# The projection and the convolution behind it eight slots later in the last unit of an attention

## Chip, cores and metric

The kernel runs on one core of one Trainium2 chip. The metric is the device time of one execution in microseconds (us); the median of three runs is given.

## What is computed

Four layers follow one another on an input of 2 images, 256 channels, 64 x 64 pixels, all in float32.

```python
x = _L0_conv_ref(x, ...)   # group norm, attention of 4 heads over 4096 pixels, projection, + xn
x = _L1_conv_ref(x, ...)   # + position term
x = _L2_conv_ref(x, ...)   # bottleneck: 1x1 conv, deformable 3x3 conv (mask), 1x1 conv, + x
x = _L3_conv_ref(x, ...)   # group norm, deformable 3x3 conv, group norm, deformable 3x3 conv, + x
```

The attention and the deformable convolution are

```python
scores = jnp.einsum('bhci,bhcj->bhij', q, k) * d ** (-0.5)
attn = jax.nn.softmax(scores, axis=-1)
out = jnp.einsum('bhij,bhcj->bhci', attn, v).reshape(B, C, H, W)
proj = jnp.einsum('bchw,oc->bohw', out, w_proj) + b_proj[None, :, None, None]
...
samp = _bilinear(h, y, x)            # 4 corners for each of 9 taps, gathered by computed offsets
out = jnp.einsum('bckhw,ock->bohw', samp, w.reshape(O, C, 9))
```

## The kernel before

**Units, blocks, slots.** The attention (`attention`, line 181) works on four units: image 0 or 1, first or second pair of heads (`units`, line 243). The last unit is image 1, second pair. A unit has 16 blocks of 256 query pixels, a block 16 slots, and a slot is one piece of work for 128 query pixels, one head and 1024 keys. So the last unit has 256 slots. The loop at line 678 takes two slots a turn. In each it sends to PE the scores of two slots ahead (`scores`, L581), the transposes of the exponentials (`turn`, L611) and the product with the values of four slots back (`attend`, L640). DVE takes the maximum (`lowest`, L593), ACT the exponential (L599); both copy the transposed results (`keep`, L628 and L630) out of two pairs of PSUM tiles.

**The order of the work.** The order on PE, ACT, DVE and POOL is that in which the code issues it. Only SP's queue of transfers is ordered by the scheduler, and a transfer may stand there ahead of those issued before it. Each engine works its queue in order: an instruction that waits holds up all behind it.

**Steps with a slot of their own.** `due(at, f)` puts a step into a slot; `small(n)` runs it there, steps of one slot in the order of their entry. For block i of a unit, with `at = 16i`, the class `Block` (line 447) enters: the softmax shares across four key parts (`compare`, `raised`, `weights`, slots 13 to 15); `spread` (16), where PE transposes the shares (L503), DVE copies them, and SP writes them to memory and reads them back as tile `f` spread over the partitions (L507, L511); and `combine` (20), where POOL multiplies the block's outputs `o` with `f` (L520), adds the parts (L521) and writes half of tile `avs` (L526). In the very last block DVE does that.

**The projection and what follows.** Every odd block also has `fetch` (17), a load of `res`; `project(0)` and `project(1)` (27 and 28), where PE multiplies `avs`, which holds two blocks, with the projection weights (L545) and DVE adds the result to `res` (L556), after which SP stores it in `xa` (L558); and, in units of the second pair of heads, `second_layer` (30): the first 1x1 convolution of the bottleneck (`Bottleneck.first`, L939 on PE, four copies `h` on ACT, L956). `make_q` (L279) stands in slot 18 of every 32 and makes the next queries, with copies to tile `qs` by SP (L289).

**Tiles with one buffer.** `f`, `avs`, `res`, `o` and `pos` have one buffer each (`o` holds the outputs of even blocks, `pos` those of odd blocks in the last unit). All steps of `small` and of the background share one PSUM bank, `pm` (`Bank`, line 43): copies out of it by ACT are put off until the next step asks for the bank or the next turn begins.

**Background.** A slot without a step of its own takes a background step, and each turn one or two more (`background`, line 662). In the last unit these are, in order of precedence: `Bottleneck.before` for image 1 (line 964), which waits until a `second_layer` has run, then makes that part of the image (PE transposes L973, SP stores L983) and the offsets of the part before (L1010, L1041 on PE, some twenty small DVE steps in `corners`, line 732); what is left of image 0's bottleneck and the building of its image (`early_image`, line 1217); and `early_samples` (line 1254), which computes offsets for five blocks of the first deformable convolution and queues 180 gathers.

**Early gathers.** At the end of each turn `self.sample()` (lines 727 and 1292) issues up to two pairs on POOL: a store of a finished gather to memory (L1297) and the next gather (L856), 512 KB each; 15 pairs fall between two combines. `combine` stands among them in POOL's queue.

**After the attention.** `deform` (line 1338) runs the bottleneck's deformable convolution of image 1 beside the first layer of the last convolution. Its loads of `xa` (L919) and of the stored samples (L1485) stand in SP's and POOL's queues.

Of the kernel before, what the change touches and what calls it, by code (L numbers as in the profile page):

```python
# [64 lines left out]
class Net:  # L65
# [115 lines left out]
    def attention(self, bott):  # L181
# [5 lines left out]
        with ExitStack() as ctx:  # L187
# [39 lines left out]
            for i in range(NB):  # L227
# [3 lines left out]
                if i == 1:  # L231
                    for j in range(2):
                        at = slice(64 * j, 64 * j + 5)
# [9 lines left out]
            units = [(b, hp) for b in range(B) for hp in range(2)]  # L243
# [154 lines left out]
            def due(at, f):  # L398
                own.setdefault(at, deque()).append(f)
# [47 lines left out]
            class Block:  # L447
# [3 lines left out]
                def __init__(self, u, i):  # L451
                    self.u, self.i = u, i
                    self.low = work.tile([P, 4, 4], F32, name="low")
                    self.sum = work.tile([P, 4, 4], F32, name="sum")
                    at = u * per_unit + 16 * i
                    due(at + 13, self.compare)
                    due(at + 14, self.raised)
                    due(at + 15, self.weights)
                    due(at + 16, self.spread)
                    due(at + 20, self.combine)  # L460
                    if i % 2:
                        due(at + 17, self.fetch)
                        due(at + 27, lambda: self.project(0))
                        due(at + 28, lambda: self.project(1))
                        if units[u][1] == 1:
                            due(at + 30, self.second_layer)
# [211 lines left out]
            while n < last + 4 or back or more or any(own.values()):  # L678
                u, d = divmod(n, per_unit)
# [1098 lines left out]
```

## Time and profile before

| | |
|---|---|
| median of 3 runs | 5222.68 us (5215.43 to 5223.12) |
| profiled execution | 5255.39 us, its span 5253.6 us |
| PE busy | 4874.5 us, 93% of the span |
| DVE, ACT, POOL busy | 76%, 63%, 47% |
| 2600 to 3075 us: PE, POOL busy | 433 us and 261 us of 475 |
| the same: DMA engines | 96% busy, 348 GB/s |
| transposes of the shares (L503) in the last unit | blocks 4, 5, 7, 9, 11, 13, 14, 15 begin at 2578.2, 2622.7, 2715.5, 2808.3, 2913.8, 3012.3, 3060.3, 3101.4 us |
| last projection (L545) | begins at 3110.6 us |

The profile takes one execution, so its times are set against its own 5255.39 us. A line of the waits names who waited, for whom, and how long in total. In a timeline, the bracket at the end of a line is the idle time before the instruction and what ended it. TensorE's clock is given as the share that was granted.

### The profile page before, as it was taken

How to read it: one execution, taken by the hardware profiler on the slowest of the kernel's cores; microseconds unless marked ns; L12 is line 12 of the kernel's file. 1: busy time of each engine (PE TensorE's matmuls, PEld its weight loads, DVE VectorE, ACT ScalarE, POOL GpSimd, SP SyncE). 2: the span in 40 equal slices, each digit the busy share in tenths (PEclk: the TensorE clock that was granted, in tenths of full speed). 3: DMA queues.
4: the chain of work that ended last, by engine and by line, in shares of the span. 5: the costliest groups of instructions: out<-in, count | busy, mean ns of one | idle time of the engine just before them, and what ended most of it. 6: DMA issues, size and time to landing. Idle time of an engine off the chain costs nothing.

```text
span 5253.6 us, 101327 instructions
## 1 busy us (share of the span) xinstructions
PE 4874.5 (93%) x38680; PEld 2736.0 (52%) x38680; DVE 3977.1 (76%) x7081; ACT 3284.2 (63%) x5941; POOL 2446.4 (47%) x2436
## 2 busy tenths in 40 slices
PE   8999999999999999989998877788999999999998
PEld 5555565555555555555555544444444544444444
DVE  6878767787678888665676757777778888888887
ACT  5676656666566666564566645557866766666665
POOL 0111101111018888622455547774766666666665
PEclk9999999999999999999999988889999999999999
DMA  4221111111113333346799988888989999999998
GB/s 167 64 94 56 44 61 44 49 30 46 50 52 104 103 107 111 102 123 210 266 346 356 343 296 276 283 299 308 345 321 322 371 334 336 336 381 345 341 356 304
DMA packets 398997, 1113.50 MB, mean 212 GB/s; under 512 B 65052, under 2 KB 102490, under 8 KB 398510
## 3 DMA queue, kind: packets, MB, share of 16 engines
q0 software_dynamic: 222480, 784.79, 41.4%
q1 hardware_dynamic: 175486, 322.11, 18.9%
q8 instruction: 303, 4.96, 0.4%
q14 instruction: 184, 1.51, 0.1%
q10 hardware_dynamic: 544, 0.13, 0.0%
HBM read 914.48 MB, written 183.97 MB: 209 GB/s over the span
## 4 chain that ended last, share of the span: by engine, by line
PE 28%; DVE 9%; DMA 8%; issue 4%; ACT 3%; another core or an unknown queue 3%; POOL 2%; DVEq 0%; SPq 0%; ACTq 0%; POOLq 0%
PE out L1564 12%; PE pd L813 4%; PE pt L1545 3%; DVE smp L1533 2%; PE av L640 2%; DVE four L1514 2%; PE sc L581 2%; DMA samp_d<-xb 2%; DMA four<-img,didx 2%; DMA xb<-img,bidx 1%; DVE smp L1527 1%; PE pm L813 1%; PE tt L611 1%; DMA samp_d<-bx 1%
## 5 line engine op out<-in xcount | busy, mean ns | idle before, releaser
L599 ACT ACTIVATE e<-sc,low 128x1024 f32<-128x1024 f32 x1024 | 1147.4, 1120 | 746.5 <-DVE low L593 704.9
L593 DVE TENSOR_REDUCE low<-sc 128x1 f32<-128x1024 f32 x1024 | 1205.3, 1218 | 247.5 <-PE sc L581 226.5
L1564 PE MATMUL out<-st,wc 128*128 128x512 f32 x2304 | 1238.7, 620 | 123.8 <-ACT st L1554 61.2
L856 POOL DMA_INDIRECT four<-img,didx x972 | 1034.5, 1064 | 613.8 <-issue 237.1
L581 PE MATMUL sc<-k,qs 64*128 64x512 f32 x2048 | 1007.4, 611 | 0.3 <-DVE k L368 0.3
L640 PE MATMUL av<-et,v 128*64 128x256 f32 x8192 | 996.1, 385 | 0.0
L581 PE MATMUL sc<-k,q 64*128 64x512 f32 x2048 | 984.7, 610 | 0.0
L611 PEld LDWEIGHTS tt<-ident,e 64*128 64x128 f32 x16384 | 655.0, 140 | 560.6 <-issue 280.1
L630 ACT COPY et<-tt 128x512 f32<-128x512 f32 x1152 | 659.5, 585 | 225.2 <-PE tt L611 164.9
L611 PE MATMUL tt<-ident,e 64*128 64x64 f32 x16384 | 733.5, 227 | 70.4 <-ACT et L630 44.5
L628 DVE COPY et<-tt 128x512 f32<-128x512 f32 x896 | 612.9, 684 | 175.4 <-PE tt L611 166.5
L640 PEld LDWEIGHTS av<-et,v 128*64 128x64 f32 x8192 | 553.1, 137 | 303.5 <-issue 50.5
L856 POOL DMA_INDIRECT bfour<-img,bidx x576 | 610.2, 1059 | 214.9 <-issue 111.8
L1545 PEld LDWEIGHTS pt<-ident,smp 128*128 128x128 f32 x2304 | 332.0, 145 | 664.4 <-issue 551.3
L1533 DVE SCALAR_TENSOR_TENSOR smp<-four,dw,smp 128x256 f32<-128x256 f32 x1296 | 626.3, 483 | 58.5 <-issue 14.3
L520 POOL TENSOR_TENSOR o<-o,f 128x1024 f32<-128x1024 f32 x48 | 113.9, 2374 | 1094.4 <-DVE o L472 542.5
L1564 PEld LDWEIGHTS out<-st,wc 128*128 128x128 f32 x2304 | 390.0, 197 | 362.7 <-issue 245.3
L1514 DVE SCALAR_TENSOR_TENSOR four<-four,dwt 128x512 f32<-128x512 f32 x540 | 403.8, 748 | 173.2 <-ACT four L1508 125.1
L1545 PE MATMUL pt<-ident,smp 128*128 128x128 f32 x2304 | 452.4, 279 | 28.2 <-DVE smp L1527 18.4
L1554 ACT COPY st<-pt 128x1024 f32<-128x1024 f32 x288 | 289.4, 1005 | 297.7 <-PE pt L1545 178.6
L581 PEld LDWEIGHTS sc<-k,qs 64*128 64x128 f32 x2048 | 349.2, 190 | 213.9 <-issue 128.3
L1508 ACT ACTIVATE four<-four,dwt 128x512 f32<-128x512 f32 x540 | 388.2, 719 | 111.6 <-DMA four<-img,didx 96.4
(201 smaller groups left out, 5416.9 us busy)
## 6 DMA issues: line engine op xcount, KB each, us to landing
four<-samp_d SPq DMA_DIRECT2D x172, 512.0 KB
samp_d<-xb POOLq DMA_DIRECT2D x116, 512.0 KB
f<-share_d SPq DMA_DIRECT2D x128, 256.0 KB
xb<-xn SPq DMA_DIRECT2D x55, 512.0 KB
img<-imgt SPq DMA_DIRECT2D x96, 256.0 KB
xa<-res SPq DMA_DIRECT2D x32, 512.0 KB
samp_d<-k POOLq DMA_DIRECT2D x32, 512.0 KB
samp_d<-bx POOLq DMA_DIRECT2D x32, 512.0 KB
```

The costliest lines, as they stand in the source:

```text
L581: nc.tensor.matmul(s[:, j, :], lhsT=q[u, i // 2][int(h != j)][halves[j], at : at + P], rhs=k[u][c][halves[j], h, :], start=True, stop=True,)
L593: nc.vector.tensor_reduce(low, s, AX.X, ALU.max, negate=True)
L599: nc.scalar.activation(e.rearrange("p j n -> p (j n)"), s, AF.Exp, bias=blk.low[:, g, c : c + 1], accum_out=blk.sum[:, g, c : c + 1],)
L611: nc.tensor.transpose(pt[:, m, :], e[half, m // 4, m % 4 * P : m % 4 * P + P], self.ident[half, half],)
L628: nc.vector.tensor_copy(dst, pt)
L630: nc.scalar.copy(dst, pt)
L640: nc.tensor.matmul(now["av"][halves[h], :], lhsT=v[u][c][:, m, halves[h]], rhs=ets[j][:, m, h, :], start=(m == 0), stop=(m == 7),)
L856: self.nc.gpsimd.indirect_dma_start(out=dst, out_offset=None, in_=img, in_offset=bass.IndirectOffsetOnAxis(ap=idx, axis=0),)
L1514: nc.vector.scalar_tensor_tensor(uv, four[:, 2 * C :], share(s, 1, 1), uv, ALU.mult, ALU.add)
L1533: nc.vector.scalar_tensor_tensor(smps[s], four[:, c], weight(s, c), smps[s], ALU.mult, ALU.add)
L1545: nc.tensor.transpose(pts[u][:, c, j * P : (j + 1) * P], smp[:, c * P : c * P + P], self.ident,)
L1564: nc.tensor.matmul(outs[ob], lhsT=wc[k][:, c, ob * P : ob * P + P], rhs=sts[u][:, c, :], start=(k == 0 and c == 0), stop=(k == K2 - 1 and ...
```

## The change

In the last unit, for the odd blocks 1 to 13, `project(0)`, `project(1)` and `second_layer` are entered at slots 35, 36 and 38 of the block instead of 27, 28 and 30. `fetch` stays at 17. Block 15 and the other units are not changed.

```diff
                     if i % 2:
                         due(at + 17, self.fetch)
+                        if u + 1 == len(units) and i < 15:
+                            at += 8
                         due(at + 27, lambda: self.project(0))
                         due(at + 28, lambda: self.project(1))
                         if units[u][1] == 1:
                             due(at + 30, self.second_layer)
```

Since slots with a step of their own take no background step there, the background moves too. Counted from the start of the last unit:

| step | slot before | slot after |
|---|---|---|
| first early offsets ready, first gather | 47 | 45 |
| block 3: project, second_layer, image part 1, offsets of part 0 | 75, 76, 78, 81, 81 to 91 | 83, 84, 86, 87, 88 to 101 |
| block 13: project, second_layer, image part 6, offsets of part 5 | 235, 236, 238, 241, 241 to 251 | 243, 244, 246, 247, 248 to 261 |
| last store of an early gather | 241 | 239 |
| block 15: project, second_layer | 267, 268, 270 | the same |

In SP's queue, the store of `xa` and the next load of `res` now follow the queries' copies (`qs`) and stand ahead of the image's four stores; the shares and `f` of the even blocks come before them.

## Prediction

> **What bounds the kernel now.** I read the list of what PE waited for first, cut to the last half of the attention (2000 to 3110 us). Its columns are us in total, times, longest.
>
> ```profile
> PE pm L545 <- POOL avs L526: 23.1, 4, 10.9
> PE tt L611 <- ACT et L630: 21.4, 22, 4.4
> PE tt L611 <- DVE et L628: 9.7, 7, 3.3
> ```
>
> The moved projection (L545) is itself the largest wait: four times PE stands still until POOL has written `avs` in `combine` (L526). The same list for POOL (2300 to 3110 us) shows why POOL is late:
>
> ```profile
> POOL xb L856 <- DMA samp_d<-xb: 81.3, 88, 3.5
> POOL samp_d L1297 <- DMA xb<-img,bidx: 75.2, 62, 3.0
> ```
>
> POOL's queue holds the 180 early gathers and stores, each waiting for a transfer, with `combine` in between. In the table of stretches (us, PE, PEld, DVE, ACT, POOL, PE clock, DMA share, GB/s) the DMA engines are full:
>
> ```profile
> 2650.00:2700.00 50.00, 45.82 (x483) 27.16 (x479) 37.24 (x57) 31.25 (x59) 27.34 (x34) 0.99 0.98 367
> 2800.00:2850.00 50.00, 38.75 (x423) 22.85 (x421) 27.36 (x39) 27.13 (x52) 28.76 (x36) 0.90 0.96 333
> ```
>
> So from about 2600 to 3075 us the DMA engines set POOL's pace, and POOL sets PE's at every projection. POOL's timeline gives odd combines beginning at 2641.9, 2740.5, 2840.8, 2940.4 and 3037.8 us: 99 us for two blocks (32 slots). PE alone is faster: its transposes of the shares (L503) for blocks 7 and 9 begin at 2715.5 and 2808.3, 92.8 us apart, of which 6.4 are waits, leaving 86.3. PE gains 12 to 13 us on POOL in two blocks and gives it back at L545. The last time it does so, in PE's timeline (start, us, work):
>
> ```profile
> 3036.60 1.95 PE L640 MATMUL av<-et,v 128*64 128x256 f32 x16
> 3042.34 1.08 PE L545 MATMUL pm<-avs,wproj 128*64 128x512 f32 x4 [3.79 <-POOL avs L526]
> 3043.35 0.85 PE L611 MATMUL tt<-ident,e 64*128 64x64 f32 x16
> 3043.99 1.17 PE L581 MATMUL sc<-k,q 64*128 64x512 f32 x1
> ...
> 3101.37 0.30 PE L503 MATMUL pm<-ident,share 128*64 128x128 f32 x1 [0.59 <-DVE share L492]
> ```
>
> and POOL's side of it:
>
> ```profile
> 3037.77 2.37 POOL L520 TENSOR_TENSOR pos<-pos,f 128x1024 f32<-128x1024 f32 x1
> 3040.22 1.26 POOL L521 TENSOR_TENSOR pos<-pos 128x512 f32<-128x512 f32 x1
> 3041.56 0.72 POOL L526 TENSOR_TENSOR avs<-pos 128x256 f32<-128x256 f32 x1
> ```
>
> POOL had no gap before this combine (its last gather ends where it begins), so 3042.3 us is set by the DMA chain, whatever PE does.
>
> **The change, step by step.** Slots count from the start of the last unit.
>
> 1. *The seven moved projections* (blocks 1 to 13) add no instruction. Before, PE cannot pass slot 16i+27 until combine(i) is done; now slot 16i+35. At 3042.3 us PE stands at slot 235 before the change; after it, PE may stand at slot 243. The eight slots between hold eight slots of attention: the pair of slots repeats every 4.79 us in PE's timeline (L640 at 3012.48, 3017.27, 3022.06) and 4.85 a little later, so 4 x 4.83 = 19.3 us. From the anchor to the last L503 (slot 256) PE took 3101.4 - 3042.3 = 59.0 us. After the change 19.3 of these are already spent: the last L503 comes at 3082.1, **19.3 us earlier**. It holds if PE can be at slot 243 by 3042.3. From block 5's L503 (slot 96, 2622.7) it is 147 slots, 4.59 x 86.3 = 396, so 3019: 23 us of room. The stalls on `et` in that stretch (4.42, 2.4, 4.19, 3.88 us at 2700, 2797, 2899, 2998) take 14.9 if they all stay, leaving 8. With two blocks at 89.7, as between blocks 9 and 11 less their waits, 15.6 more goes, PE is 7.5 late, and this step gives 12. I take enough room: 19.3.
>
> 2. *What is late next.* POOL falls up to 15 slots behind its place in the program, 7 before. The next things that hold PE for a late combine are `o`/`pos`, rewritten by DVE for block i+2 some 19 slots after combine's place: four slots are left. `avs` in the other direction: combine(i+1) writes it after project(1) of block i, now in combine's own slot, and before it in that slot. Combines 6, 8 and 10 began at 2692, 2792 and 2891 us, when PE by the rate above is past the projection by over 10 us. I cost it at nothing; if that cover went, POOL would wait at most one projection (1.1 us) in seven blocks.
>
> 3. *The one bank `pm`.* The projection now follows make_q (slots 18, 19 of 32) and the image step follows the second layer (22, 23), so each waits for a copy on ACT put in between. Before, the transpose of the shares paid for the h copies: 3.0 us in five waits, 0.3 to 1.0 each; the next row for a q or k copy is 0.7 us (L503 on ACT k L427). The four h copies take 1.97 us together. Bounds per block are -1.0 (the old wait is gone and the new one hidden by the attend matmuls) and +2.7; I take +0.5, the nearest row being the old wait. All but the last of these fall where PE has room, so 0.5 us counts.
>
> 4. *Background work and POOL.* Of 32 slots, 11 and 12 come free for background steps (14 keeps `raised`) and 19 and 22 are taken (20 already holds combine): as many steps, but ahead of the image they wait for. The early samples' first block is ready at slot 45, not 47, and their last store stands at 239, not 241. POOL waits for PE's products at combines 2 and 3 anyway (14.4 and 26.6 us), so the two pairs done earlier fall off the end: two pairs are 2 x (3075 - 3042)/13, some 5 us. The chain of gathers ends near 3070.
>
> 5. *SP's queue.* Between the f loads of block 13 and 14 stand the first two loads of the later convolution (L919), which wait for the last sample stores:
>
> ```profile
> 3019.97 1.17 SPq L511 DMA_DIRECT2D f<-share_d  x2
> 3078.05 0.38 SPq L919 DMA_DIRECT2D bx<-xa  x1
> 3078.54 0.41 SPq L558 DMA_DIRECT2D xa<-res  x1
> ```
>
> In the new order the shares and f of block 14 come straight behind them, ahead of xa, res and the image. With L919 at 3070, shares 3070.5, f issued 3074 and landed by 3079, combine(14) ends at 3083.5. The shares of block 15 leave at 3083 to 3084, f lands by 3090, DVE's combine takes 2.4 us (1.23 + 0.69 + 0.42 in its rows), and the last projection begins at 3092 to 3093 instead of 3110.6: **18 us earlier**. The unmoved last block means the image, offsets and gathers after it keep their order. A stored xa lands up to eight slots later but is loaded only in the later convolution.
>
> 6. *Other traffic.* Eight slots more of PE's loads and stores fall before the anchor: a quarter of some 3 MB for two blocks, 0.75 MB, at 350 GB/s 2 us, from 0 to 2. I take 1.
>
> Sum: 18 - 0.5 - 1 = 16.5, rounded **17 us**. Everything after the attention hangs on that last projection in the chain of waits, so it moves as a whole. The profiled run took 5255.4 us (span 5253.6): 5238 after. The median of the runs shown is 5222.7, 32.7 below it; I take the same 17 off: **5206 us**.
>
> TensorE's clock speaks for a little more. After the wait of 3.8 us the score matmuls take 1.06 us instead of 0.59; eight of them, two at a time, lose 8 x 0.47 / 2, some 2 us, and the granted clock is 0.90 in the stretch of the longest wait. The Trainium skill, "TensorE: Matmul & The Clock Gate", What's actually happening, says that an idle window of about 3.4 us halves the clock and a busy one restores it. By that rule each such wait that goes away is worth about 1.7 us more, an estimate from that page, and the sum would be 17 to 24; the trace agrees in size. I leave the gain out of the sum: by the 23 us of room, waits may stay at blocks 11 and 13, with their slow stretch.
>
> **Rivals.**
>
> *PE becomes the bound (gain 0 to 10).* DVE's 128x72 steps of the offsets take 0.23 us, and long where they meet POOL's combine:
>
> ```profile
> 2691.52 2.92 DVE L764 TENSOR_TENSOR floor<-floor,whole 128x72 f32<-128x72 f32 x1
> ```
>
> The three long `et` waits follow such meetings. The steps now lie six to ten slots later and POOL seven later, so they meet again, and spread over eight slots instead of four they can meet twice. Twice 14.9 us, with 86.3 for two blocks, overdraws the room by 23.5 - 29.8 = -6: gain 11; with 89.7 as well the gain is nil. The Trainium skill, "SBUF — State Buffer", Who interferes with whom, says that a DVE step with two SBUF inputs and a GpSimd step that reads SBUF shut each other out for a whole instruction. The 2.92 us beside POOL's 2.38 agree; by it this rival costs no more than one combine, 4.4 us, a meeting.
>
> *SP's queue turns into the wait (slower).* `f` has one buffer, so f of block i+1 waits on SP for combine(i), asked for at slot 16i+32. PE may now be three slots past that, and the q copies (qs) stand right behind. They are asked for at slot 19 of 32 and needed at 30: 11 slots, 30 us. f landed 5 to 8 us after its issue at blocks 4 and 14. It decides from a landing of 30 us on; four q blocks 7 us late each lose the 17 and 11 more: 5234. Against it: the longest landing SP itself waited for was 8.9 us.
>
> *The gain is not passed on (0).* The later convolution could be held by something that does not move, such as the sample stores. Against it: these end near 3070. It gives 5223.
>
> *More (22 to 28).* PE meets no late combine at all, and the four slow stretches of some 2 us go too: 17 + 8 = 25, so 5198.
>
> **How the numbers follow.** Forecast (gain 11 to 22) 0.60; PE the bound 0.18; not passed on 0.08; SP's queue 0.09; more 0.05. A measurement of this kernel tells a change from none at about 0.2%, 10.4 us. Faster takes the forecast, the last rival and 0.02 of PE the bound: 0.67. Same takes the rest of that and the case of no gain: 0.24. Slower 0.09. The range leaves out SP's queue and the far half of the last rival; its ends are a gain of 27 and one of 1: 5196 to 5222.
>
> **What would show it.** L545 waits for `avs` under 15 us in all, and later than block 9. The last L503 near 3082, the last L545 near 3093, the last sample store near 3070, combines still 99 us apart by two blocks. PE's wait on `et` growing past 25 us would mean the first rival, a wait of L581 on `qs` the second. If combines change pace, the DMA chain was not the bound and the anchor is wrong.

## The result, and the profile after

The median of eight executions of the changed kernel is 5202.0 us (5183.9 to 5209.7), that of the kernel before in the same set 5222.9 us (5214.5 to 5235.6). The ratio is 0.996, interval 0.9948 to 0.9973: 20.9 us less. In a second set the same pair gave 0.9956 (0.9942 to 0.9969), 20.8 us less. The profiled execution took 5197.2 us, its span 5195.3.

The two profiled executions differ by 58 us, almost three times what the medians do. Only part of that is the change: the last projection (L545 before, L547 after, the new code being two lines further down) begins at 3110.6 us before and 3087.8 after, 22.8 us earlier. Behind it the one took 2143.0 us and the other 2107.5, but another profiled execution of the unchanged kernel took 2111.0 there. So the 22.8 us are read below, and the rest is left alone.

PE's waits after the change, 2000 to 3110 us (us in total, times, longest):

```profile
PE tt L613 <- ACT et L632: 14.4, 20, 2.2
PE pm L547 <- POOL avs L528: 10.2, 2, 5.8
PE pm L975 <- ACT h L958: 9.6, 7, 1.7
PE tt L613 <- DVE et L630: 8.3, 8, 1.7
```

The wait of the projection for POOL is down from 23.1 to 10.2 us, in two places instead of four: it is gone at blocks 7 and 9 and left at 11 and 13. The waits for `et` fell (31.1 to 22.7 us in all) instead of growing. A new line is the image step (L975), which waits for the copies `h`.

The same two stretches as in the prediction (us, PE, PEld, DVE, ACT, POOL, PE clock, DMA share, GB/s):

```profile
2650.00:2700.00 50.00, 48.68 (x513) 28.42 (x510) 32.30 (x49) 33.91 (x65) 26.86 (x32) 1.00 1.00 360
2800.00:2850.00 50.00, 50.00 (x557) 29.67 (x555) 38.03 (x57) 35.08 (x66) 27.99 (x35) 1.00 0.97 352
```

PE is full where it was busy 38.75 of 50 us, its granted clock there is 1.00 instead of 0.90, and the DMA engines are as full as before. (The two waits that are left, at 2935 and 3033 us, lie outside this stretch.) POOL's busy time is nearly the same: PE got ahead, POOL did not. PE's timeline at the last projections (start, us, work; in the bracket the idle time ahead and its cause):

```profile
2941.23 1.98 PE L547 MATMUL pm<-avs,wproj 128*64 128x512 f32 x4 [5.82 <-POOL avs L528]
...
3036.99 1.51 PE L547 MATMUL pm<-avs,wproj 128*64 128x512 f32 x4 [4.38 <-POOL avs L528]
...
3077.43 0.30 PE L505 MATMUL pm<-ident,share 128*64 128x128 f32 x1 [1.16 <-DVE share L494]
...
3087.81 1.98 PE L547 MATMUL pm<-avs,wproj 128*64 128x512 f32 x4 [5.19 <-DVE avs L528]
```

The anchor, the projection of block 13 let go by POOL, is at 3037.0, and the last shares (L505, L503 before) at 3077.4: 40.4 us where it was 59.0. POOL's timeline around it:

```profile
3032.43 2.36 POOL L522 TENSOR_TENSOR pos<-pos,f 128x1024 f32<-128x1024 f32 x1
...
3036.21 0.72 POOL L528 TENSOR_TENSOR avs<-pos 128x256 f32<-128x256 f32 x1
...
3055.09 0.57 POOL L1299 DMA_DIRECT2D samp_d<-bx  x1 [2.86 <-issue]
...
3062.10 0.53 POOL L1299 DMA_DIRECT2D samp_d<-xb  x1 [3.95 <-DMA xb<-img,bidx]
3073.64 2.36 POOL L522 TENSOR_TENSOR o<-o,f 128x1024 f32<-128x1024 f32 x1 [11.01 <-DMA f<-share_d]
```

No gap stands ahead of the combine of block 13, as before. The combine of block 14 (the last line) waits 11 us for its `f`, and SP's queue tells why:

```profile
2991.75 1.16 SPq L513 DMA_DIRECT2D f<-share_d  x2
3059.58 1.41 SPq L921 DMA_DIRECT2D bx<-xa  x2
3061.10 0.50 SPq L509 DMA_DIRECT2D share_d<-shares  x1
3068.85 1.09 SPq L513 DMA_DIRECT2D f<-share_d  x2
```

The loads of the later convolution (L919 before, L921 after) hold everything behind them until the last early store out of tile `bx` (issued at 3055.09) has landed 4.5 us later. The shares of block 14 go out right behind.

### The profile page after: what moved, and what is told of

It reads as the page before. It is cut to its first block, busy times and chain, and to the rows that moved or that the text cites. A ratio compares the mean times of both kernels' runs of the same rounds, so it can differ in the third digit from the quotient of the medians.

```text
span 5195.3 us, 101328 instructions
## 1 busy us (share of the span) xinstructions
PE 4853.1 (93%) x38680; PEld 2726.4 (52%) x38680; DVE 3970.8 (76%) x7081; ACT 3283.0 (63%) x5941; POOL 2448.6 (47%) x2436
## 4 chain that ended last, share of the span: by engine, by line
PE 27%; DMA 9%; DVE 8%; issue 5%; ACT 3%; POOL 2%; another core or an unknown queue 2%; SPq 0%; DVEq 0%; ACTq 0%; POOLq 0%
PE out L1566 12%; PE pd L815 5%; PE pt L1547 3%; DMA samp_d<-bx 2%; DVE smp L1535 2%; DMA samp_d<-xb 2%; DVE four L1516 2%; DMA four<-img,didx 2%; DVE smp L1529 1%; PE av L642 1%; DMA xb<-img,bidx 1%; PE sc L583 1%; PE pm L815 1%; DMA bx<-img,bidx 1%
## 5 line engine op out<-in xcount | busy, mean ns | idle before, releaser
L1566 PE MATMUL out<-st,wc 128*128 128x512 f32 x2304 | 1223.3, 613 | 88.2 <-ACT st L1556 48.0
L583 PE MATMUL sc<-k,qs 64*128 64x512 f32 x2048 | 1003.7, 609 | 0.3 <-DVE k L368 0.3
L583 PE MATMUL sc<-k,q 64*128 64x512 f32 x2048 | 985.9, 608 | 0.0
L1535 DVE SCALAR_TENSOR_TENSOR smp<-four,dw,smp 128x256 f32<-128x256 f32 x1296 | 625.9, 483 | 57.6 <-issue 20.8
L1547 PE MATMUL pt<-ident,smp 128*128 128x128 f32 x2304 | 447.9, 277 | 22.0 <-DVE smp L1529 17.2
L583 PEld LDWEIGHTS sc<-k,qs 64*128 64x128 f32 x2048 | 348.0, 189 | 214.0 <-issue 125.8
```

What stands on the lines that cost most here:

```text
L583: nc.tensor.matmul(s[:, j, :], lhsT=q[u, i // 2][int(h != j)][halves[j], at : at + P], rhs=k[u][c][halves[j], h, :], start=True, stop=True,)
L1535: nc.vector.scalar_tensor_tensor(smps[s], four[:, c], weight(s, c), smps[s], ALU.mult, ALU.add)
L1547: nc.tensor.transpose(pts[u][:, c, j * P : (j + 1) * P], smp[:, c * P : c * P + P], self.ident,)
L1566: nc.tensor.matmul(outs[ob], lhsT=wc[k][:, c, ob * P : ob * P + P], rhs=sts[u][:, c, :], start=(k == 0 and c == 0), stop=(k == K2 - 1 and ...
```

## Experiments

**The theory.** POOL's chain of combines and early gathers sets the pace, at the speed of the DMA engines. PE is tied to it by the projection, and the change lets PE go eight slots further before it has to stop for POOL. **Rival one:** the gain comes from the moved convolution, image and gathers (the background's new order). **Rival two:** PE was the bound anyway, and less waiting moves nothing. A third cause came up on the way: the wait in SP's queue.

All positions below are counted from the first transposition of shares of the last unit in the same execution (2298.2 us before, 2297.3 after), since the sets differ: the medians of the kernel before are 5222.9, 5243.1, 5107.3 and 5226.4 us in the four sets. Ratios are to the kernel before of the same set. Two profiled executions of one kernel put the last projection 6.4 us (before) and 6.8 us (after) apart, so a single position is good to some 7 us. What follows the last projection differs too, by up to 11 us between the kernels of one of the three later sets, so a position is not yet a time. None of the kernels leaves work out.

| kernel | ratio (95%) | last shares (PE) | last store out of `bx` | last projection | shares to projection |
|---|---|---|---|---|---|
| before | 1 | 803.1 | 775.9 | 812.4 | 9.3 |
| before_again | one run | 809.4 | 781.2 | 818.8 | 9.4 |
| after | 0.9960 (0.9948 to 0.9973) | 780.2 | 757.8 | 790.5 | 10.3 |
| after_again | 0.9956 (0.9942 to 0.9969) | 786.3 | 762.3 | 797.3 | 11.0 |
| conv_only | 1.0002 (0.9985 to 1.0019) | 805.1 | 768.2 | 815.3 | 10.2 |
| shift4 | 1.0004 (0.9992 to 1.0017) | 806.2 | 769.2 | 816.1 | 9.9 |
| shift16 | 0.9968 (0.9954 to 0.9982) | 764.2 | 756.6 | 787.6 | 23.4 |
| dve_odd | 0.9947 (0.9928 to 0.9965) | 760.4 | 761.5 | 790.8 | 30.4 |
| early_two | 0.9993 (0.9984 to 1.0002) | 798.4 | 756.8 | 808.0 | 9.6 |
| late_two | 0.9982 (0.9973 to 0.9991) | 785.9 | 778.9 | 809.4 | 23.5 |
| before_free | 1.0001 (0.9988 to 1.0015) | 806.9 | 782.2 | 816.2 | 9.3 |
| late_two_free | 0.9962 (0.9949 to 0.9975) | 795.8 | 781.7 | 805.7 | 9.9 |
| shift16_free | 0.9949 (0.9932 to 0.9965) | 759.2 | 752.4 | 772.0 | 12.8 |
| dve_odd_free | 0.9919 (0.9905 to 0.9932) | 752.4 | 755.6 | 765.8 | 13.4 |

Two strands run into the last projection. PE's: it comes 9 to 13 us after the last shares, where nothing else holds it. SP's: it comes 29 to 33 us after the last store out of `bx`, where the shares and `f` of blocks 14 and 15 stand behind the loads of L919 and wait (late_two 30.5, shift16 31.0, dve_odd 29.3). The later one decides. In the changed kernel the two come close together: the projection is 10.3 us behind the shares and 32.7 behind the store.

### Only the convolution moved

An edit to the kernel before; the projections stay at slots 27 and 28:

```diff
-                            due(at + 30, self.second_layer)
+                            due(at + 30 + 8 * (u + 1 == len(units) and i < 15), self.second_layer)
```

> The projections stay at slots 27 and 28; only the second layer (the 1x1 convolution) moves, from 30 to 38, and with it the image and offset steps, which fall into nearly the same slots as in the changed kernel. Theory (the eight slots of slack between POOL's combine and PE's projection are the whole gain): PE waits for avs at L545 stay near 23 us in all, time within 4 us of the kernel before. Rival (the gain comes from the later convolution and the shifted background, for instance from offsets that no longer collide with POOL's combine): 12 to 20 us faster, as the changed kernel.

The ratio is 1.0002. PE's waits, in the same stretch:

```profile
PE pm L545 <- POOL avs L526: 34.4, 4, 9.7
```

All four waits of the projection are there, and no less long (23.1 and 32.3 us in the two executions of the kernel before). Rival one falls: the part that moves the convolution and the background is worth nothing by itself.

### Four slots, and sixteen

Both are edits to the changed kernel. Four slots:

```diff
-                            at += 8
+                            at += 4
```

> Four slots later instead of eight. Theory: the anchor is the combine of block 13, whose time the transfers set; four slots of attention are 9.7 us, so the last projection comes 9 to 12 us earlier than before, and 10 to 12 us earlier than in no other way; PE still waits for avs at three or four projections. Rival (any slack breaks the lockstep, so the gain is all or nothing): the same 20 us as eight slots, or none.

The ratio is 1.0004: no gain, where 9 to 12 us were expected. Its waits:

```profile
PE pm L547 <- POOL avs L528: 15.5, 3, 9.1
PE pm L505 <- DVE res L558: 10.0, 7, 1.6
```

The wait for POOL falls, but a new one appears. With four slots the second half of the projection shares slot 16i + 32 with the next block's transposition of the shares, which needs the bank `pm` and waits for DVE to add the projection to `res`, seven times. Shares that leave later make combines that begin later: block 4's is 5.6 us later, block 13's 6.7 (against before_again 6.2, but only 0.7, so the second is within the spread). That would take away most of what the four slots bring, 9.7 by the prediction's rate. From the projection of block 13 to the last shares PE then took 55.4 us, where 59.0 less 9.7 was expected: 6.1 us more. Half of that is waiting: PE was idle for 5.95 us of the stretch, 2.87 in the kernel before. The other half is slower work: PE was busy 49.45 us, where 46.4 is the middle of before (56.23) and after (36.57), with a granted clock of 0.92 (before 0.97, after 0.96). Why the clock was lower there is open, so the miss is shown in part.

For sixteen slots `avs` must hold out longer, so every second one is kept in columns of a weight tile that are free by then:

```diff
-                            at += 8
+                            at += 16
...
-                        Block.avs = one.tile([P, 512], F32, name="avs")
+                        if self.u + 1 == len(units) and self.i % 4 == 2:
+                            Block.avs = wqkv[:, 0, C:]
+                        else:
+                            Block.avs = one.tile([P, 512], F32, name="avs")
```

> Sixteen slots later; the second of each two avs tiles lies in columns of the weight tile that the last unit no longer reads, so that a combine does not overwrite an avs still to be projected. Theory: the two waits for avs left in the changed kernel (10.2 us) and their slow clock (some 4 us) go, but the last projection can come only 0 to 5 us earlier than in the changed kernel, since the shares of blocks 14 and 15 wait in SP's queue behind the two loads that wait for the last sample stores; so 20 to 26 us faster than before. Rival (the gain grows with the slack as long as POOL is late): 8 more slots, 19 us more, 35 to 40 us faster than before.

No projection waits for POOL any more, and PE reaches the last shares 16 us before it does in the changed kernel. The last projection comes only 2.9 us earlier, within the spread, and the time is not lower: 0.9968, or 15.6 us below the kernel before, where 20 to 26 was expected. PE's timeline of this kernel:

```profile
3061.54 0.30 PE L505 MATMUL pm<-ident,share 128*64 128x128 f32 x1 [2.53 <-ACT h L961]
...
3084.89 1.97 PE L550 MATMUL pm<-wqkv,wproj 128*64 128x512 f32 x4 [6.63 <-DVE pos L760]
```

Now 23.4 us lie between them instead of 10.3: PE is there and something else is late. That is the SP strand, 31 us behind the store out of `bx`. (PE's wait is put down to a later DVE step, but DVE's last combine, which had waited for `f`, ends only at 3084.2.)

### POOL taken off PE's path

Odd blocks of the last unit are combined on DVE, five slots later, and the projection stays at its old slot; the edit is to the kernel before:

```diff
-                    due(at + 20, self.combine)
+                    self.dve = u + 1 == len(units) and i % 2 == 1
+                    due(at + 25 if self.dve and i < 15 else at + 20, self.combine)
...
-                    end = self.u + 1 == len(units) and self.i == 15
-                    engine = nc.vector if end else nc.gpsimd
+                    engine = nc.vector if self.dve else nc.gpsimd
```

> The kernel before with the combine of the odd blocks of the last unit on DVE, in slot 25 instead of 20; the projections stay at 27 and 28. Theory (PE waits because combine stands in POOL's queue among the gathers): PE no longer waits for POOL's avs at L545; 12 to 25 us faster than before, less what seven DVE steps of 2.4 us cost PE through the softmax (0 to 14 us). Rival (the place of the projection in PE's own order is what matters): no gain, or slower by the DVE work, some 17 us.

The ratio is 0.9947, 27.5 us, a little more than the 12 to 25 expected, though the projection keeps its old place. PE's waits (2000 to 3130 us):

```profile
PE pm L545 <- DVE avs L526: 26.0, 1, 26.0
```

One wait of the projection is left, 26 us at the last one, and the last shares are 42.7 us earlier than before. So rival two falls: PE by itself is some 40 us faster than POOL allowed. And again 30.4 us lie between the shares and the projection.

### The early blocks alone, the late blocks alone

The change made for blocks 1 and 3 (early_two), and for blocks 11 and 13 (late_two), beside the whole of it once more in the same set (after_again):

```diff
-                        if u + 1 == len(units) and i < 15:
+                        if u + 1 == len(units) and i < 4:
```

```diff
-                        if u + 1 == len(units) and i < 15:
+                        if u + 1 == len(units) and 10 < i < 15:
```

> The changed kernel once more, on the chip of the next three. The last projection begins near 3088 us again, and combine of block 13 comes 443 us after that of block 4, as in every kernel profiled so far (443 to 445 us, 450 where block 5's combine waited for f). If the gain of some 21 us belongs to the change and not to one chip, it is 0.3 to 0.5% here too.

> Only blocks 1 and 3 are moved by eight slots. Theory: project and second layer of block 3 then no longer stand ahead of block 4's shares, which start POOL's chain; combine of block 4 begins about 5 us earlier (near 2589), the chain of 443 us follows, and the projections of blocks 7 to 13 wait for avs as before, some 20 us or more in all. So the last projection comes 4 to 7 us earlier and the time falls by that. Rival (the slack at the late blocks is everything and the start counts nothing): 0.

> Only blocks 11 and 13 are moved by eight slots. Theory: POOL's chain is as before (combine of block 13 ends near 3042), PE waits at blocks 7 and 9 as before, and can be eight slots further when block 13's combine is done: 72 slots from block 9's projection at 2845 take 194 us by 86.3 for 32 slots, so 3039. The last projection comes 15 to 19 us earlier, though only two of seven projections move. Rival (every moved projection gives its own part of the gain): two sevenths of 21, some 6 us.

The whole gains 20.8 us, the early blocks 3.7 (the interval reaches 0; 4 to 7 was expected), the late blocks 10.9. In after_again the last projection came at 3082.2 us and the chain from combine 4 to combine 13 took 450.6 us, where 3088 and 443 were expected. By the anchor alone the late blocks should have brought nearly everything, 15 to 19 us. PE does arrive earlier, 785.9 against 803.1, but the projection of this one execution hardly does (809.4 against 812.4). PE's timeline of late_two:

```profile
3069.87 0.30 PE L505 MATMUL pm<-ident,share 128*64 128x128 f32 x1 [0.59 <-DVE share L494]
...
3093.38 1.98 PE L547 MATMUL pm<-avs,wproj 128*64 128x512 f32 x4 [18.81 <-DVE avs L528]
```

PE stands 18.8 us at the last projection. SP waits twice in a row ahead of the two loads, first for the gather into `bx` and then for the store out of it. These are the two waits in the kernel before, in the changed kernel and in late_two:

```profile
SPq L919 <- DMA bx<-img,bidx: 52.7, 1, 52.7
SPq L919 <- DMA samp_d<-bx: 4.0, 1, 4.0
...
SPq L921 <- DMA bx<-img,bidx: 42.9, 1, 42.9
SPq L921 <- DMA samp_d<-bx: 23.6, 1, 23.6
...
SPq L921 <- DMA bx<-img,bidx: 67.7, 1, 67.7
SPq L921 <- DMA samp_d<-bx: 3.7, 1, 3.7
```

SP's timeline of late_two:

```profile
3066.51 0.88 SPq L921 DMA_DIRECT2D bx<-xa  x2
...
3072.26 1.09 SPq L513 DMA_DIRECT2D f<-share_d  x2
...
3083.15 1.13 SPq L513 DMA_DIRECT2D f<-share_d  x2
```

SP stood 71.4 us ahead of L921, and everything behind it, `f` of blocks 14 and 15 too, went late. In the kernel before it was 56.7 us, after the change 66.5: there SP stands longer but gets away sooner (3059.6 instead of 3078.1), since it comes to these loads earlier and the store out of `bx` is done earlier. The early blocks do the other half: in early_two the last store out of `bx` is 19 us earlier than before, but PE's last shares are not. Only the whole change moves both strands.

### The load taken out of SP's queue

The first two loads of the later convolution's input go to POOL's queue, where the gathers that they wait for have been issued already. Done to the kernel before (before_free), to late_two, to shift16 and to dve_odd (each with _free); before_again is the kernel before, unchanged:

```diff
-        def block(self, pool, src, i):
+        def block(self, pool, src, i, queue=None):
...
-            self.net.nc.sync.dma_start(
+            (queue or self.net.nc.sync).dma_start(
...
-                    x = self.block(pools["x"], net.xa_d[b], i)
+                    x = self.block(pools["x"], net.xa_d[b], i, nc.gpsimd if b and i < 2 else None)
```

> The kernel before, for a profile on the chip of the next three. Counted from the shares (L503) of the last unit's first block, the last L503 begins near 803 us, the last projection near 812, and combine of block 13 comes 443 us after that of block 4, as in the first profile.

> The kernel before, with only the first two loads of the later convolution's input on POOL's queue instead of SP's. Theory (the attention ends when both PE and POOL's chain with the f loads behind it are done, and before the change PE is the later of the two): the last L503 stays near 803 us after the last unit's first, the last projection near 812; 0 to 3 us faster. Rival (SP's queue was the bound all along, and what dve_odd_free gained over dve_odd belongs to this edit alone): 12 to 25 us faster.

> Blocks 11 and 13 moved by eight slots, and the two loads on POOL's queue. Theory: with only these blocks moved PE was at the last L503 17 us earlier, but the last projection came only 3 us earlier (809 us after the last unit's first L503), since f of blocks 14 and 15 stood behind the two loads. With both edits it comes at 795 to 799; 13 to 20 us faster than before, though the second edit alone gives nothing. Rival (the two edits add up: 11 measured for the one and what the other gives alone): no more than 11 to 14.

> Sixteen slots later, and the two loads on POOL's queue. Theory: PE reached the last L503 at 764 us after the last unit's first and the gathers ended there too, but the last projection began at 788. With f of block 14 free, combine 14 follows the last store at once and the last projection begins at 776 to 780: 8 to 12 us faster than with sixteen slots alone, 25 to 30 us faster than before. Rival (what was left is PE's own work): no gain over sixteen slots, 17 us.

> The kernel with the odd combines on DVE, with the first two loads of the later convolution's input on POOL's queue instead of SP's. Theory: in that kernel PE was at block 15's shares at 3060 and then waited 26.0 us at the last projection, because f of block 14 stood in SP's queue behind these two loads, which wait for the last sample stores. Without them f of block 14 lands before the gathers end (3061), combine 14 ends near 3066, f of block 15 lands by 3073 and the last projection begins at 3075 to 3078 instead of 3090.7: 12 to 16 us faster than the kernel it is made from, some 38 to 42 us faster than before. Rival (the wait comes from POOL's own gathers and from the f transfers under load, not from SP's order): 0 to 4 us.

The unchanged kernel, before_again, came with its last shares at 809.4 and its last projection at 818.8, and its chain took 450.1 us; 803, 812 and 443 were expected. Such is the spread of two executions.

Alone, on the kernel before, the edit gains nothing (1.0001): there PE is the later strand. With the other strand out of the way it pays. In dve_odd the gain goes (between two sets) from 27.5 to 47 us, in shift16 from 15.6 to 27, in late_two from 10.9 to 17. The intervals of each pair overlap (dve_odd narrowly: 0.9928 to 0.9965 against 0.9905 to 0.9932), so it is the trace that carries this: the stretch from shares to projection falls from 23 to 30 us to 9.9 to 13.4 in all three. The last projection comes 25.0 us earlier in dve_odd and 15.6 in shift16, further than expected in both, and 3.7 in late_two, which is within the spread. PE's timeline of dve_odd_free:

```profile
3039.06 0.30 PE L504 MATMUL pm<-ident,share 128*64 128x128 f32 x1 [0.59 <-DVE share L493]
...
3052.47 1.97 PE L545 MATMUL pm<-avs,wproj 128*64 128x512 f32 x4 [9.08 <-DVE avs L526]
```

and its SP queue, where `f` of block 14 leaves 34 us before the last shares instead of waiting for the last store:

```profile
3005.24 1.10 SPq L512 DMA_DIRECT2D f<-share_d  x2
```

late_two_free missed its expectation for the position: the last projection at 805.7, where 795 to 799 was expected. The wait on SP is gone (9.9 us after the shares), but PE itself came later (795.8 against 785.9), with longer waits for `et` and 207.6 us for the 72 slots from block 9's projection to block 13's, where 194 was reckoned and late_two took 199.3. Of these 8.3 us, 4.1 are waits for `et` (8.1 against 4.0) and 4.2 a longer busy time of PE (197.6 against 193.4), with a granted clock of 0.97 against 0.99. Why both were worse is open. dve_odd_free is the fastest of all: 0.9919, 47 us below the kernel before of its set and 26 below the changed kernel. The changed kernel itself was not run with these loads moved.

## Why the prediction was right, step by step

The forecast was 17 us and 5206 us; 20.9 us and 5202.0 us were measured, the last projection 22.8 us earlier where 18 was worked out.

1. *The anchor and the eight slots* held. From the projection of block 13 to the last shares PE took 40.4 us instead of 59.0: 18.6 us, forecast 19.3; in the second execution of each, 42.6 instead of 59.2. The odd combines begin at 2638.1, 2738.6, 2835.2, 2936.7 and 3032.4 us, 98.6 us apart for two blocks, forecast 99. In the two executions each of the kernel before and of the changed one, the nine steps from combine 4 to combine 13 take 443 to 451 us, and 439 to 451 in all twelve executions that leave these combines on POOL, however far ahead PE is. conv_only shows that the projection's place is what counts. The room was smaller than the 23 us worked out: in the changed kernel PE waited for POOL only 5.8 and 4.4 us, 10.2 in all, near the 8 that were left if the stalls on `et` all stayed.

2. *The term that was mis-sized is the anchor itself*, which I held fixed at 3042.3 us. It came at 3037.0, 4.4 us earlier relative to the unit's start (739.7 against 744.1). The chain keeps its pace but begins earlier: the combine of block 4 is at 2589.3 instead of 2594.3, and the shares of block 4, which it needs, are transposed at 2570.1 instead of 2578.2. Before, they stood behind block 3's projection and convolution in PE's order; now these come after them. My step 4 counted the background's move at the end of the chain and not this one at its start. 18.6 + 4.4 gives 23 us for the last shares (803.1 to 780.2). The projection then came about 1 us later behind them, and the whole unit had begun 1 us sooner, so that it is 22.8 counted from the start of each execution. That the chain begins earlier repeats: combine 4 begins 288.6 to 292.1 us into the unit in after, after_again and early_two, and 295.5 to 298.6 in before, before_again, before_free, late_two and late_two_free. How much of it reaches the anchor is not settled. The 4.4 us lie within the spread of two executions, the early blocks alone gain 3.7 us with an interval that reaches 0, and in conv_only combine 4 begins at 289.2 but the nine steps take 450.1 us and nothing is gained.

3. *Nothing next in line* (`o`, `pos`, `avs` the other way) shows as a wait, as costed.

4. *The bank.* I took +0.5 us a block for the image step's wait on the copies `h`. It is 9.6 us in seven, 1.4 each, for 3.0 in five before: about 1 us a block more, inside the bounds. It lies where PE has to wait for POOL anyway.

5. *SP's queue.* I saw the block of the loads (L919) and had it end near 3070; it ended at 3059.6. The last early store came at 3062.1 (764.8, against 775.9 before), 11 us earlier and not 5. And the loads wait for the last store out of `bx` alone, one of five buffers in turn: it was the last store of all before, and the turn ends three stores further on after the change, so `bx` is free 7 us sooner. That second part I had not seen. It mattered: with PE's part alone (late_two) the last shares come 17.2 us earlier, but the time falls by only 10.9, and I had this queue as a step that merely follows. The rival "not passed on" names the sample stores as what could hold the later convolution. It did not come true because they moved as well; had only PE's strand moved, it would have in part, as in late_two.

6. *Other traffic*, 1 us, cannot be told apart in the traces.

*The rivals.* PE as the bound: its waits on `et` did not pass 25 us but fell to 22.7, and dve_odd shows PE with 40 us in hand. SP's queue by way of `qs`: no wait of L583 on `qs` shows. The case of more, without any late combine: waits stay at blocks 11 and 13, as I had it. The case's slow stretches stay with them: the projection after the 5.82 us wait takes 1.98 us, where the one behind the 3.79 us wait that the prediction shows took 1.08.

*The clock.* I had left its gain out of the sum. The Trainium skill, "TensorE: Matmul & The Clock Gate", What's actually happening, led to an estimate of up to 24 us. The granted clock did go from 0.90 to 1.00 in the stretch of the longest wait, as by that rule. But behind the anchor PE gained 18.6 us, not more than the slots account for. A faster clock ahead of a wait would only lengthen the wait; no run here changes the clock alone, so this part is argued and not shown.

## What to carry to other kernels

Where a slow queue paces a fast engine through one wait, moving the waiting step later buys at most the work that stands in between, once, and not a faster pace; find the last place where the two meet, and count from there. Before costing such a gain, look for a second strand that ends at the same point (here a load that stands too early in an in-order queue), because the smaller of the two leads is the gain. An edit that measures nothing by itself, like before_free, may be what makes the next one pay.

## What the runs showed of the hardware

**A load in an in-order queue waits for its buffer with all that stands behind it.** SP stood 56.7 us before, 66.5 after and 71.4 in late_two ahead of two loads for the later convolution, while the shares of block 14 waited behind them.

**A small DVE step can take as long as a POOL instruction.** In the changed kernel the conversion of the offsets to integers, 0.18 us in the median of eleven, took 3.04 and 2.90 us where it met POOL's combine of 2.37 us (in after_again the longest is 1.18). The first of the two in DVE's timeline:

```profile
2887.07 3.04 DVE L778 TENSOR_SCALAR bidx<-whole 128x36 int32<-128x36 f32 x1
```

POOL's instruction runs from 2887.69 to 2890.06, and the DVE step ends at 2890.11 with it. The prediction had this for a step with two inputs; here it has one.

**One kernel's median differs by 136 us between sets**, 5107 to 5243, while its ratio to another kernel repeats within 0.0004 (0.9960 and 0.9956). The three sets with experiments ran on three chips. The mean granted clock goes with the time: 0.982 to 0.983 in the profiled executions of after_again, early_two and late_two in the fastest set, 0.971 to 0.974 in those of the slowest. Most of the difference lies behind the attention. Between after and after_again, the same kernel, the profiled spans differ by 106.6 us, and 101.0 of these lie behind the last projection. There the DMA engines moved 335 and 352 GB/s, at granted clocks of 0.95 and 0.97. Which of the two makes the difference is not shown.
